# Holding the convolution for one period at the end of the last batch's mixing, and shifting it by one period from there on

## The chip, the cores and the metric

The kernel runs on one core of a Trainium2 chip. The metric is the device time of one execution in microseconds (us): the median of several runs. A profiled execution beside them gives the trace from which all durations below are read. Engines: PE is TensorE, DVE VectorE, ACT ScalarE, POOL GpSimd, SP the engine that issues nearly all DMAs here.

## The reference

The input `x` has 4 images of 256 x 256 positions and 64 channels, in float32. Layer 0 is a residual block, layer 1 a linear map along the image height:

```
h  = layernorm(x) @ w_te                          64 -> 128 channels
F  = fft2(h);  fc = gelu([Re F, Im F] @ w_fc)      the mixing, 256 -> 256
x1 = x + real(ifft2(fc)) @ w_tp                    128 -> 64
d  = gelu(depthwise_conv3x3(layernorm(x1) @ w_fe)) the convolution
x2 = x1 + d @ w_fp
out = moving average of x2 over the height + filtered rest   (layer 1)
```

Layer 1 is linear in the height and has its own weights per channel, so the kernel builds one 256 x 256 matrix for each channel and multiplies.

## The kernel before

**Stages.** The forward part turns columns of `x` into partial transforms and spills them to DRAM. The spectral part ("mixing") reads these, 65 pairs of frequencies per batch, transforms along the width, applies the weights and the gelu, projects, turns the result, and transforms back along the width (`u`, `us`, `uc`, `uf`: lines 849 to 924), which spills tensors `u_d` to DRAM. The convolution takes a batch in 32 chunks of 8 columns: it loads `uc` from `u_d` (`ul` or, for a batch's first chunk, `UL`, line 968) and a chunk of `x` (`xl`, line 1025), transforms back along the height (`s`, line 1034), adds to `x` (`r0`, `r1`), normalises (`c*`), turns to channels (`t`, `tt`), forms row sums on POOL (`T0`, `T1`), multiplies by the convolution weights (`gm`, `gh`, `em`, `eh`: lines 1166 and 1180), combines on DVE (`gc_`, `cf`, `ce`), applies the gelu (`a`), projects (`o`), turns back (`ft`) and stores (`st`, line 1314). Layer 1 follows when the last chunk is stored.

**Order.** The order of the instructions on PE, DVE, ACT and POOL is written out by hand; each engine runs its list in order. Time is cut into periods, numbered `n`. In each period the function `period` (line 1679) goes through a written list of pairs `operation:offset` and calls `do(operation, n + offset)`; `do` (line 1636) first calls what the operation depends on (`FOLLOWS`), so an operation that is asked for early pulls its predecessors forward, and one that was done already does nothing. There are four lists: `SPECTRUM`, `FULL` (forward, mixing and convolution), `MIXED` (mixing and convolution) and `CONV` (convolution alone, from period `CONV_FROM` = 171). SP's queue is not in these lists: its order is put together when the program is built.

**Chunks and periods.** `chunk_at` (line 1540) gives each chunk an index; in period `n` an operation with offset -k works on the chunk with index `n - k`. A convolution chunk is in flight for about 7 periods. A batch's first chunk needs the whole batch mixed, so it is set at `S0 + opened(b) + 2 + LATE` at the earliest. In numbers: batch 2 has the indices 137 to 168, batch 3 (the last) 170 to 201, and index 169 belongs to no chunk. Below, chunks 26 to 31 are those of batch 2, and 0', 1', 2' and so on those of batch 3. In period 169 the operations with offset 0 find no chunk, in period 170 those with offset -1, and so on to offset -6 in period 175: each stage skips once, one after the other.

**Late chunks.** From index `LATE_CHUNKS` = 167 (chunk 30) on, the products for the outer rows stay in PSUM and DVE adds them (`ce0`, `ce1`, line 1250). Earlier chunks have ACT copy them out (`ec`, line 1195) and POOL add (`sp`, line 1214).

**The end of the mixing.** The last two back transforms along the width, `u` with the numbers 131 and 132, stand in the periods 168 and 169. Their results are finished by `uf` 132 and `uf` 133 (one DVE instruction each, lines 920 and 907, and two DMAs each), which `UL` of chunk 0' calls in period 170. `UL` then loads the first columns, `first_column` (line 990) adds to them on DVE, and `s` of 0' (line 1041) reads them.

Of the kernel before, what the change touches and what calls it, by code (L numbers as in the profile page):

```python
# [136 lines left out]
def conv_seq_kernel(ctx: ExitStack, tc: tile.TileContext, a: dict, tables: bass.AP, out: bass.AP):  # L137
    nc = tc.nc
    x = a["x"]
    B = x.shape[0]  # L140
# [11 lines left out]
        em="ec1", o0="fs0", o1="fs1", ft0="st0", ft1="st1", y0="yt0", y1="yt1",  # L152
# [15 lines left out]
    def make_room(op):  # L168

        for other in list(taken):  # L170
            if len(free_banks) >= NEEDS.get(op, 1):
                break
            if other in taken:
                holder, k = taken[other][1]
                late = holder == "em" and k >= LATE_CHUNKS
                releaser = "ce1" if late else RELEASES[holder]
                if (releaser, k) not in pulling:
                    pulling.append((releaser, k))
                    do(releaser, k)
                    pulling.pop()  # L180
# [1299 lines left out]
    def x2_load(pool, c, b0, bufs):  # L1480
        xc = pool.tile([P, 2, BH, N // SW, CG, SW], F32, tag="xc", name=f"xc_{c}_{b0}", bufs=bufs)
        for b in range(BH):
            for t in range(2):
                nc.sync.dma_start(
                    xc[:, t, b], x2_d[b0 + b, t * P : (t + 1) * P, c // CG]
                )
        return xc
# [45 lines left out]
    S0 = FWD + 3  # L1533
    LATE = 1

    def opened(b):

        return (KH * (b + 1) + 2) // 2 + 1

    chunk_at, at = {}, 0  # L1540
    for b in range(B):
        at = max(at, S0 + opened(b) + 2 + LATE)
        for q in range(COLS):
            chunk_at[at] = (b, q)
            at += 1
    END = at + 6
    place = {chunk: at for at, chunk in chunk_at.items()}
    CONV_FROM = S0 + LATE + opened(B - 1) + 3

    def is_late(j):  # L1550
        return place[j] >= LATE_CHUNKS

# [21 lines left out]
    def numbered(text):  # L1574

        return [(w.split(":")[0], int(w.split(":")[1]) if ":" in w else 0) for w in text.split()]

    follows = {}
    for line in FOLLOWS.replace("\n", "|").split("|"):
# [15 lines left out]
    MIXED = numbered("""  # L1595
        xl:-1 XL:-1 ft0:-6 zs:-5 st0:-6 ft1:-6 st1:-6 em:-4 g0:-3 T1:-3 Ta:-3 eh:-4 zt:-6 ec0:-4
        ec1:-4 m1:-3 sp0:-5 sp1:-5 cx:-2 w:-5 cf1:-5 gc1:-3 g1:-4 b1:-3 cm:-1 cc:-2 UL t0:-2 a0:-5
        xs:-1 zt:-5 gm:-4 t1:-2 tt0:-2 a1:-5 p0:-4 p1:-4 z:-4 zs:-4 gh:-4 uf:-3 cM:-1 p0:-3 gc_0:-4
        cf0:-4 g1:-3 cp:-1 m1:-2 gc1:-2 b1:-2 s cl tt1:-2 r0 gc_1:-4 m0:-2 gc0:-2 m0:-1 p1:-3 z:-3
        gc0:-1 r1 x b0:-2 xs o1:-5 fs1:-5 u:-2 o0:-5 T0:-2 x:1 cq b0:-1 us:-2 fs0:-5 g0:-2 cr cR  # L1600
        uc:-2 w:-4 ul:1
    """)
# [4 lines left out]
        cm:-1 cc:-2 cM:-1 cp:-1 cf0:-4 tt1:-2 cf1:-4 tt0:-2 em:-4 eh:-4 T0:-2 T1:-2 cx:-1 fs1:-5 UL  # L1607
    """)

    LATE_CHUNKS = CONV_FROM + max(at for op, at in MIXED if op in ("em", "gm"))  # L1610

    FIRST = numbered("""
        v:1 mm:-2 fl:1 fM fr fm y0:-2 y1:-2 v:2 mm fq:1 fx:-1 fp fh1:-1 fh0:-1 fm:1 vc:1 yt0:-2 fq:1
# [22 lines left out]
    def do(op, index):  # L1636

        if op not in ops:
            return
        for k in range(done.get(op, -1) + 1, index + 1):  # L1640
            for other, at in EARLY.get(op, ()) if k < LATE_CHUNKS else ():
                do(other, k + at)
            for other, at in follows.get(op, ()):
                do(other, k + at)
            if op in ("u", "zt") and ring[0](op, k):
                do(*ring[0](op, k))
            if op in ("fq", "cq", "cc") and sq_user:
                user = sq_user[-1][0]
                do(user, done[user[0] + "q"])
            if op in RELEASES:  # L1650
                make_room(op)
            if done.get(op, -1) >= k:
                continue
            done[op] = k
            busy.append((op, k))
            if op in PAIRS:
                if op == "x" and k < B * KH - 2:
                    do("yt0", (k + 3) // KH * FWD + FWD - 1)
                    do("yt1", (k + 3) // KH * FWD + FWD - 1)
                if k < B * KH:  # L1660
                    ops[op](k)
            elif op in BACK:
                ops[op](k)
            elif op in MATRICES:
                if k < C:
                    ops[op](k)
            elif op in HALF_MATRICES:
                if k < 2 * BESIDE:
                    ops[op](k)
            elif op in forward:  # L1670
                if k < B * FWD:
                    ops[op](k)
            elif k in chunk_at:
                if op == "UL" and chunk_at[k][1] == 0:
                    do("uf", opened(chunk_at[k][0]) + 1)
                ops[op](chunk_at[k])
            busy.pop()

    def period(n):
        if any(n - k in chunk_at for k in range(7)):  # L1680
            names = FULL if n < B * FWD + 4 else MIXED if n < CONV_FROM else CONV
        else:
            names = SPECTRUM
        joint["on"], joint["whole"] = names is FULL, names is SPECTRUM
        for op, at in names:
            base = n
            if op in PAIRS:
                base = 2 * (n - S0)
            elif op in BACK:
                base = n - S0  # L1690
            elif op in HALF_MATRICES:
                base = (n - S0 - HALF_MATRICES[op]) // 2
            do(op, base + at)

    def starting(n, prep):
# [6 lines left out]
    with in_order, ExitStack() as right:  # L1702
        with (
# [3 lines left out]
            forward = forward_h(fwd)  # L1707
# [3 lines left out]
            with ExitStack() as early:  # L1711
                pool = early.enter_context(tc.tile_pool(name="matrices", bufs=2, side="right"))
                prep = early.enter_context(tc.tile_pool(name="prep", bufs=1, side="right"))
                ops |= matrices(pool)
                do("fl", 1)
                nc.sync.dma_start(tab, tables[:, :_L0_END])
                pieces = prepare(prep)
                next(pieces)
                nc.sync.dma_start(b_fp, row(a["b_fp"]).to_broadcast([P, C]))
                for n in range(S0 // 2):  # L1720
                    starting(n, pieces)
                for _ in pieces:
                    pass
                do("yt0", FWD - 1)
                do("yt1", FWD - 1)
                load_group(0)
                for k, names in enumerate(BETWEEN, C - BESIDE - len(BETWEEN)):
                    do("v", k)
                    do("vc", k)
                    do("mt", k - 1)  # L1730
                    for op, at in names:
                        do(op, S0 - 1 + at)
                do("mt", C - BESIDE - 1)
                begin(0)
                ops |= spectrum
                early_end = S0 + 4 * BESIDE + 1
                for n in range(S0, early_end):
                    if n == early_end - 3:
                        give_back()
                    period(n)  # L1740
# [4 lines left out]
            for n in range(early_end, S0 + LATE + opened(B - 1) + 2):  # L1745
                period(n)
        with tc.tile_pool(name="seq", bufs=1, side="left", reuse_waits="tile") as seq:
            mts = [matrix_load(seq, c) for c in range(0, CG, CM)]
            xc = x2_load(seq, 0, 0, 1)
            for n in range(S0 + LATE + opened(B - 1) + 2, END):  # L1750
                period(n)
            right.close()
            with tc.tile_pool(name="seq2", bufs=1, side="right", reuse_waits="tile") as seq2:
                for c in range(0, C, CG):
                    if c:
                        mts = [matrix_load(seq, c + i) for i in range(0, CG, CM)]
                    for b0 in range(0, B, BH):
                        if c or b0:
                            xc = x2_load(seq2, c, b0, 3)
                        layer1(c, b0, mts, xc, seq)  # L1760
# [39 lines left out]
```

## Time and profile before

| what | value |
|---|---|
| runs | 4324.39, 4318.21, 4323.12 us; median 4323.12 |
| profiled execution | 4325.4 us, of which the span of the trace is 4323.6 |
| busy over the span | PE 96%, DVE 80%, POOL 73%, ACT 68% |
| granted TensorE clock | 0.984 of full speed over the span |

A view by stretches gives the busy time of each engine between two times of the span. A timeline lists instructions that stand together: start, duration, engine, line, operation, tiles, and in square brackets how long the engine stood idle before and what ended that. A line of the matmuls of `s`, line 1041, marks each period: chunk 30's starts at 3290.64 us, 31's at 3313.56, 0's of the last batch at 3360.50.

### The profile page before, as it was taken

The numbers are of one execution on the slowest core, as the hardware profiler recorded it, in microseconds if no ns is written. First come the engines' busy times: TensorE is split into PE (matmuls) and PEld (weight loads), VectorE is DVE, ScalarE is ACT, GpSimd is POOL, SyncE is SP. The second block draws the span as 40 slices with busy tenths as digits, with TensorE's granted clock in tenths as the row PEclk, the third lists the DMA queues.
The fourth block names the chain that finished last, engine by engine and source line by source line (L and its number), as shares of the span: only waits on it lengthen the run. The fifth ranks groups of instructions, "written<-read, shape, count | busy, mean of one in ns | idle before, by whom it ended". The sixth has DMA issues, their size and how long they took to land.

```text
span 4323.6 us, 67389 instructions
## 1 busy us (share of the span) xinstructions
PE 4158.0 (96%) x22443; PEld 2315.2 (54%) x22443; DVE 3453.4 (80%) x5234; ACT 2961.5 (68%) x5409; POOL 3163.4 (73%) x3156
## 2 busy tenths in 40 slices
PE   8999999899999999899999999999998899999999
PEld 4544444345555555455555566666665566654444
DVE  6968999779999998899999878888887799962222
ACT  3338998678888887788888777888885466641111
POOL 6869999688888887788888877888887588840000
PEclk9999999989999999999999999999999999999999
DMA  6664555535454544444444443344433544439995
GB/s 190 211 190 142 161 161 162 152 98 137 137 137 137 137 137 124 122 122 138 138 138 129 113 109 109 106 112 112 118 98 91 173 113 118 114 108 358 342 343 228
DMA packets 763906, 655.28 MB, mean 152 GB/s; under 512 B 46413, under 2 KB 657695, under 8 KB 755240
## 3 DMA queue, kind: packets, MB, share of 16 engines
q1 hardware_dynamic: 726696, 583.84, 46.5%
q10 hardware_dynamic: 36864, 67.13, 4.1%
q8 instruction: 180, 2.95, 0.3%
q14 instruction: 166, 1.36, 0.1%
HBM read 364.81 MB, written 286.00 MB: 151 GB/s over the span
## 4 chain that ended last, share of the span: by engine, by line
PE 42%; POOL 6%; DVE 4%; DMA 4%; ACT 3%; issue 1%; SPq 1%; ACTq 0%; POOLq 0%; DVEq 0%
PE ps_o L1504 9%; PE ps_h_c L1166 5%; PE ps_p L750 3%; PE ps_s_c L1041 3%; PE ps_h_c L1180 3%; PE ps_f_c L1283 3%; PE ps_hh_c L1166 2%; PE ps_z L805 2%; PE ps_t_c L1088 2%; PE ps_u L856 2%; PE ps_x L725 2%; PE ps_ft_c L1308 2%; DMA out_dram<-oc 1%; PE ps_zt L823 1%; POOL xb L609 1%
## 5 line engine op out<-in xcount | busy, mean ns | idle before, releaser
L770 DVE TENSOR_TENSOR g<-ps_p,g 128x512 f32<-128x512 f32 x1040 | 702.2, 683 | 127.9 <-ACT g L764 109.7
L781 POOL TENSOR_TENSOR g<-g 128x512 f32<-128x512 f32 (+1 forms) x520 | 677.9, 1315 | 98.5 <-ACT g L775 88.8
L775 ACT ACTIVATE g<-g,b_fc 128x1024 f32<-128x1024 f32 (+1 forms) x520 | 598.3, 1151 | 1.5 <-DVE g L770 1.4
L750 PE MATMUL ps_p<-xs,wp 64*128 64x512 f32 (+1 forms) x2080 | 561.1, 615 | 9.9 <-DVE g L770 2.7
L1166 PE MATMUL ps_h_c<-td,wc_main 128*128 128x256 f32 x2048 | 517.1, 391 | 7.3 <-DVE s_c L1234 0.8
L764 ACT COPY g<-ps_p 128x512 f32<-128x512 f32 (+1 forms) x520 | 298.0, 585 | 268.5 <-PE ps_p L750 101.1
L1504 PE MATMUL ps_o<-xc,mt 128*128 128x512 f32 x1024 | 443.3, 595 | 3.9 <-DVE oc L1518 3.8
L1166 PEld LDWEIGHTS ps_h_c<-td,wc_main 128*128 128x128 f32 x2048 | 370.1, 193 | 122.5 <-ACT zt L833 36.7
L1276 ACT ACTIVATE h_c<-h_c,b_conv 128x1024 f32<-128x1024 f32 x256 | 297.6, 1164 | 140.6 <-DVE h_c L1245 54.1
L1518 DVE TENSOR_SCALAR oc<-ps_o,b_fp 128x512 f32<-128x512 f32 x128 | 93.5, 749 | 351.4 <-DMA out_dram<-oc 196.7
L1516 ACT ACTIVATE oc<-ps_o,b_fp 128x512 f32<-128x512 f32 x128 | 86.2, 686 | 363.0 <-PE ps_o L1504 196.7
L1128 POOL TENSOR_TENSOR td<-tt 128x512 f32<-128x512 f32 x256 | 327.0, 1299 | 10.0
L1504 PEld LDWEIGHTS ps_o<-xc,mt 128*128 128x128 f32 x1024 | 195.3, 191 | 251.2 <-issue 236.0
L609 POOL TENSOR_TENSOR xb<-xt 128x512 f32<-128x512 f32 x224 | 285.4, 1282 | 54.5 <-DVE xt L602 41.1
L750 PEld LDWEIGHTS ps_p<-xs,wp 64*128 64x128 f32 x2080 | 189.3, 186 | 239.6 <-issue 84.7
L805 PE MATMUL ps_z<-g,w_tp 128*64 128x512 f32 x1024 | 288.7, 617 | 24.6 <-POOL g L781 19.9
L725 PEld LDWEIGHTS ps_x<-tab,yb 128*64 128x64 f32 x4064 | 235.0, 138 | 133.3 <-issue 69.2
L1322 DVE TENSOR_TENSOR st<-x_c,ps_ft_c 128x256 f32<-128x256 f32 x512 | 261.8, 602 | 44.4 <-PE ps_ft_c L1308 41.4
L615 PE MATMUL ps_y<-xb,tab 128*64 128x512 f32 x1024 | 273.4, 623 | 23.3 <-POOL xb L609 17.1
L1283 PE MATMUL ps_f_c<-h_c,w_fp 128*64 128x512 f32 x1024 | 266.3, 615 | 15.6 <-ACT h_c L1276 15.5
L1180 PE MATMUL ps_h_c<-td,wc_half 64*128 64x256 f32 (+1 forms) x2048 | 278.6, 396 | 2.4 <-POOL td L1132 1.1
L1041 PE MATMUL ps_s_c<-uc_c,tab 64*128 64x512 f32 x1024 | 259.6, 616 | 15.6 <-DVE uc_c L990 8.7
(201 smaller groups left out, 9559.4 us busy)
## 6 DMA issues: line engine op xcount, KB each, us to landing
y_d<-yt SPq DMA_DIRECT2D x256, 256.0 KB, 3.6
yb<-y_d SPq DMA_DIRECT2D x256, 256.0 KB, 4.0
u_d<-ut SPq DMA_DIRECT2D x256, 256.0 KB, 3.6
x_c<-in_x_dram SPq DMA_DIRECT2D x512, 128.0 KB, 3.6
x_d<-st SPq DMA_DIRECT2D x128, 512.0 KB, 5.1
xc<-x_d SPq DMA_DIRECT2D x64, 1024.0 KB, 8.5
out_dram<-oc ACTq DMA_DIRECT2D x256, 256.0 KB, 5.8
xt<-in_x_dram SPq DMA_DIRECT2D x504, 128.0 KB, 2.5
```

What stands on the lines that cost most here:

```text
L609: engine.tensor_tensor(sums[j][:, i], x0, x1, (ALU.add, ALU.subtract)[i])
L750: nc.tensor.matmul(ps[:, :nf], wp[rows, cols], rhs[rows], start=True, stop=r == 1 or not pr["special"],)
L770: nc.vector.tensor_tensor(gt[:, i], re, gt[:, 1], op)
L775: nc.scalar.activation(g, g, AF.Gelu, bias=b_fc[:, half : half + 1])
L781: nc.gpsimd.tensor_tensor(g[:, 0], g[:, 0], g[:, 1], op)
L805: nc.tensor.matmul(ps[r * C : (r + 1) * C, :nf], w_tp, d[:, :nf], start=True, stop=True)
L1041: nc.tensor.matmul(pss[i], tb[i * C : (i + 1) * C], uc[i * C : (i + 1) * C, ::-1, 1 - r, :] if down else uc[i * C : (i + 1) * C, :, r, :], ...
L1128: tt_(new[:, k : k + 3 : 2], a_c, nb_e, op)
L1166: nc.tensor.matmul(product(j, k, par), wc_main[:, par, k, :], td[:, k, slots(j)].rearrange("p j q -> p (j q)"), start=k in (0, 1, 3), stop ...
L1180: nc.tensor.matmul(product(j, k, par)[:, dst.start * Q : dst.stop * Q], wc_half[lo : lo + C, k, :], td[lo : lo + C, k, src].rearrange("p j ...
L1283: nc.tensor.matmul(ps[par * C : (par + 1) * C], w_fp, gs[j][:, :, par, i0 : i0 + 2, :].rearrange("p r j q -> p r (j q)"), start=True, stop ...
L1504: nc.tensor.matmul(ps[:, :nf], mts[i // CM][:, i % CM, t, to * P : (to + 1) * P], xc[:, t, :, :, i, :], start=t == 0, stop=t == 1,)
```

## The change

A list `HOLDS` is added with one period in it, 36 + 132 = 168. In that period and in all later ones the operations of the convolution are called with the index `n - 1 + offset` in place of `n + offset`; those of the forward part, the mixing and the matrices keep theirs. So in period 168 every operation of the convolution is asked for a chunk that it did in period 167, and nothing of the convolution is issued. The chunks of batch 3 get the indices 169 to 200, with no free index before them, so their operations stand in the same periods as before: `s` of 0' in period 170. The chunks of batch 2 that are in flight in period 168 do each of their remaining steps one period later. `LATE_CHUNKS` becomes 166: chunk 29 is now treated as a late one. `END` stays 208.

```diff
+    HOLDS = [S0 + LATE + opened(B - 1)]
     chunk_at, at = {}, 0
     for b in range(B):
-        at = max(at, S0 + opened(b) + 2 + LATE)
+        at = max(at, S0 + opened(b) + 2 + LATE - sum(n <= S0 + opened(b) + 2 + LATE for n in HOLDS))
         for q in range(COLS):
             chunk_at[at] = (b, q)
             at += 1
-    END = at + 6
+    END = at + 6 + len(HOLDS)
...
-    LATE_CHUNKS = CONV_FROM + max(at for op, at in MIXED if op in ("em", "gm"))
+    LATE_CHUNKS = (
+        CONV_FROM - len(HOLDS) + max(at for op, at in MIXED if op in ("em", "gm"))
+    )
...
     def period(n):
-        if any(n - k in chunk_at for k in range(7)):
+        if any(n - k in chunk_at for k in range(7 + len(HOLDS))):
             names = FULL if n < B * FWD + 4 else MIXED if n < CONV_FROM else CONV
...
                 base = (n - S0 - HALF_MATRICES[op]) // 2
+            elif op not in forward:
+                base = n - sum(held <= n for held in HOLDS)
             do(op, base + at)
```

What this makes of the engines' lists, read from the two built programs (up to chunk 30's `s`, and again from chunk 5' on, they are the same):

- PE: the eight matmuls of `u` 131 come right after those of `u` 130, and `u` 132 takes 131's old place, between the `o` matmuls of chunk 26. `s` of 0' follows the products of chunk 28; before it followed those of 29. From there to 5' each period has all stages, in the order `s, ft, gm, ft, o, gh, t, t, em, eh`; before, the stages of the missing index were absent one by one.
- DVE: the first `uf` instruction of `u` 130 (line 920) and the two of `uc` 131 come before the `st` of chunk 25; lines 920 and 907 of `uf` 132 and 133 come right after the variance of chunk 31. Chunk 29 gets four instructions of `ce`.
- ACT: `us` 131 comes before the boundary copy (`Ta`, line 1138); two copies (`ec`) of chunk 29 are gone. POOL: four additions (`sp`) of chunk 29 are gone.
- SP: the stores of `uf` 130, 131, 132 and 133 each move forward; the store of `st` 12 and the load of `x` for 31 stand around those of 130 and 131. In the refill, the load of chunk 1' now stands wholly after the store of `st` 13; four loads of layer 1's matrices (0.5 MB each) stand together ahead of the load of `x` for 2', and the small store `fix_d` stands between the two halves of that load.

## The prediction

> **What bounds the kernel now.** I read the page first. Its row of slices (each about 108 us) shows PE at 90% or more nearly everywhere, and low in two neighbours, slices 31 and 32, from 3243 to 3459 us.
>
> ```profile
> span 4323.6 us, 67389 instructions
> ...
> PE   8999999899999999899999999999998899999999
> ```
>
> That is where the mixing ends and the last batch's convolution starts. The view by stretches, cut at the starts of `s` (line 1041), comes next; its columns are stretch, length, then busy time and count of PE, PE's weight loads, DVE, ACT, POOL, then granted clock and DMA.
>
> ```profile
> 3223.74:3246.50 22.76, 22.76 (x150) 14.68 (x150) 19.10 (x29) 19.07 (x35) 19.00 (x23) 1.00 0.22 62
> 3290.64:3313.56 22.92, 18.42 (x91) 12.15 (x89) 14.69 (x24) 10.48 (x22) 14.43 (x21) 0.85 0.44 115
> 3313.56:3360.50 46.94, 34.75 (x171) 22.93 (x167) 28.11 (x46) 20.92 (x41) 27.91 (x34) 0.89 0.37 102
> 3360.50:3444.88 84.38, 68.27 (x336) 42.88 (x338) 63.42 (x113) 36.84 (x72) 50.24 (x82) 0.90 0.56 181
> 3444.88:3514.20 69.32, 68.59 (x396) 47.08 (x394) 66.07 (x119) 43.23 (x83) 57.34 (x84) 1.00 0.39 107
> ```
>
> With mixing a period takes 22.8 us and PE is full. After the mixing's pairs are done (3290 on) it still takes 22.9 with no engine full: the written order, not work, sets it. From chunk 0' to 5' (3360.50 to 3444.88) five periods take 84.4 us though their stages are thinned out; the next five, complete, take 69.3, PE full and DVE at 95%. The timeline of PE shows the waits inside.
>
> ```profile
> 3304.50 1.12 PE L1088 MATMUL ps_t_c<-ident,xn_c 128*128 128x128 f32 x4 [3.33 <-POOL xn_c L410]
> 3305.41 3.62 PE L1166 MATMUL ps_h_c<-td,wc_main 128*128 128x256 f32 x8
> ...
> 3349.11 1.11 PE L1088 MATMUL ps_t_c<-ident,xn_c 128*128 128x128 f32 x4 [3.75 <-POOL xn_c L410]
> ...
> 3360.50 3.01 PE L1041 MATMUL ps_s_c<-uc_c,tab 64*128 64x512 f32 x8 [2.28 <-DVE uc_c L990]
> ...
> 3404.43 3.68 PE L1283 MATMUL ps_f_c<-h_c,w_fp 128*64 128x512 f32 x8 [5.77 <-ACT h_c L1276]
> ```
>
> Each period waits some 3.3 us for POOL's `xn`, and the matmuls after it run at half speed (3.62 us; the same eight take 1.89 at 3298). The chain of waits (start, duration, what) tells what 0' waited for.
>
> ```profile
> 3347.92 0.60 DVE h_c L1245
> 3348.51 1.63 DVE ut L920
> 3350.16 0.61 SPq L896
> 3350.82 3.69 DMA u_d<-ut
> 3355.05 4.71 DMA first<-u_d
> 3359.86 0.55 DVE uc_c L990
> 3360.50 2.95 PE ps_s_c L1041 x7
> ```
>
> So the last mixing result goes DVE line 920, store, load, line 990, `s`: 12.0 us, and its start is set by DVE's list, behind the combine of chunk 28.
>
> [...]the shortest `x` load takes 2.7 us to land, and SP's loads of line 1030 did stand for the buffers of `st`.
>
> **The change, step by step.** All times are in the profiled execution's span.
>
> *The hold.* Before, period 168 cost a whole 22.92 us row of convolution. In the new list it holds `u` 131, `us`, `uc` and `uf` 130 only. PE: +1.72 us (eight matmuls of line 856) after 3296.0. There PE stood 1.17 us for `fs` anyway, so `ft` of 25 comes 0.6 late, and chunk 27's products end at 3301.7 in place of 3301.2; then PE waits for `xn` 29 until 3304.5, which POOL makes from inputs that are long ready. Net on PE: 0. DVE: line 920 (1.1) and `uc` (1.3) now stand ahead of `st` 25, which starts at 3300.4 in place of 3298.0; behind it stand the combine of 26 (ends 3306.2, was 3303.9), the variance, line 907 and the seed (3308.6, was 3306.3). What waits for these: ACT's gelu of 26 and the `tt` copies behind it (to 3309.8; ACT was next needed at 3312.95), and POOL's ten small operations, 3308.7 to 3311.7 (POOL was next needed at 3314.67). SP: the `x` load of 31 has its second half behind the store of 131, issued about 3310, landing about 3314, wanted at 3315.5. So `s` of 31 still starts at 3313.6: the hold costs nothing while these covers of 1.5 to 3 us stand, at most about 2.5 us if they don't.
>
> *The chain to 0'.* `u` 132 now stands where 131 stood (3316.28). DVE reaches the variance of 31 at 3326.76 as before and then line 920 of `uf` 132 at 3327.9, where line 907 stood; before it was 3348.4. The 12.1 us behind it are the same instructions and DMAs with the same neighbours: `s` of 0' at 3340.0 in place of 3360.5. Gain 20.5 us. One period of about 22 us is gone, and nothing that it did is left out: it goes into the refill.
>
> *The refill.* Before, 0' to 5' took 84.4 us: 68.3 of PE, part of that at half clock (granted 0.90). New matmuls in it: the stages of one chunk, `t` 1.1, products 7.6, `o` 1.9, `ft` 0.9, about 11.5 us; the idle is 16.1. Period by period: (1) 0' to 1' was 19.86; now the transposes of 31 stand in it, +1.1: 20.9. (2) 1' to 2' was 15.19, set by DVE, whose list there (13.4 us, plus nine instructions of the first chunk, about 1.9) is unchanged: 15.2. (3) 2' to 3' is a complete period: 13.9, from the rows after 3444 (69.3 / 5). (4) 3' to 4' has chunk 31, whose gelu waits for the edge addition (line 1269). Before, `o` came 8.9 us after `s` (3395.55 to 3404.43); a complete period has 6.3 us of matmuls between (3444.88 to 3451.18), so 2.6 us stay: 16.5. (5) 4' to 5' has the edge of 0': 3427.20 to 3435.72, 8.5, less 6.3: 16.1. Sum 82.6; gain 1.8. Chunk 29 as a late one puts 1.6 us on DVE in (1), behind 29's combine and ahead of `r0` of 1', which by this count is then 1 us late; POOL loses 2.9 us and ACT 1.1, which were not on the path. From 5' on the lists are the same, and layer 1 starts when the chunks end, so what is gained stays.
>
> *Sum.* 20.5 + 1.8 = 22.3 us. The profiled execution, 4325.4, becomes 4303.1; that one is 2.3 above the median of the runs, 4323.1, which becomes **4300.8 us**.
>
> Unknown: how PE's clock falls in the refill. At best all five periods take 13.9 and (1) 20.9: 76.5, gain 28; at worst the 11.5 us of added matmuls find no idle: 84.4 + 11.5, gain 9. I take the middle because the waits of (4) and (5) are in the trace.
>
> **Rivals.** *Loads come late (gain 10 to 15).* Layer 1's first 6 MB (four matrices, four 1 MB loads of `xc`) are issued at about 3335 to 3341. `x` of 1' is now issued wholly behind `st` 13's store, about 3356, wanted at 3362.5; two loads of 2' stand behind `fix_d`, about 3374, wanted at 3379. For it: `x` loads took up to 13.7 us to land between 3355 and 3400, with a median of 5.2. Against: by 3356 the 6 MB, at the 417 GB/s of the stretch 3360 to 3370, are 15 us gone. Price about 8 us, and a restart at half clock: 4310.
>
> *The refill is full (gain 28):* 4295. For it: PE has enough matmuls to keep its clock. Against: the edge chunks.
>
> *Nothing is gained.* The chain to 0' doesn't set the end; the thinned stages had slack that paid for the wait, so a full refill gives back what the hold saves: the added matmuls plus stalls of 10 us. 4321. Against: PE stands idle 16.1 us there, and DVE 21.
>
> *Slower: the clock stays down.* A PE that idles 4.6 us before `s` of 0' and 2.5 in (4) and (5) may run the refill at a low clock. At a granted 0.66, the worst 10 us stretch of before (3400 to 3410), instead of full speed, 62 us of matmuls after 1' cost 32 more: -22.3 + 32, 4333. It turns the sign below about 0.74 over the whole refill. Against: each fall in the trace is over in 3.6 us, and the thinner refill had 0.90.
>
> **How the numbers follow.** Likeliest (4295.5 to 4307) 0.60; late loads (4307 to 4314) 0.17; full refill (4290 to 4295.5) 0.09; nothing gained (4314.5 to 4331) 0.09; slower 0.05. A measurement here can tell about 0.2%, 8.6 us, from no change: faster, below 4314.5, is 0.86, same 0.09, slower 0.05. The range leaves out half of the full refill and the last two: 4292 to 4315.
>
> **What would show it.** `s` of 31 at the same time as before, 3313 to 3316: the hold is free. `s` of 0' near 3340, after a chain with line 920 at 3328. From 0' to 5' 80 to 86 us, PE's idle mostly ahead of line 1283 twice. `s` of 5' near 3422.6, and a period of 13.9 from there. Wrong if `s` of 31 slips by 3 us or more, if `r0` (line 1054) waits for DMAs, or if PE's clock in the refill is under 0.85.

## The result, and the profile after

| | before | after |
|---|---|---|
| median of 8 runs each | 4320.48 us (4318.21 to 4324.39) | 4304.24 us (4294.02 to 4307.89) |
| profiled execution | 4325.4, span 4323.6 | 4307.88, span 4306.1 |

The ratio of the times is 0.9959, with a 95% interval of 0.9948 to 0.9969: 16.2 us are gained, where 22.3 were forecast. The profiled executions differ by 17.5. The time lies in the forecast range, 3.4 us above the predicted 4300.8. The gain is short by more than that, by 6.1 us, because before's own median over eight runs is 2.6 us lower than that over the three from which the forecast started.

The page of the changed kernel, its span and PE's row of slices:

```profile
span 4306.1 us, 67386 instructions
...
PE   8999999989999999899999999999998899999999
```

The low pair is still in slices 31 and 32, so the page can't say what happened there. The view by stretches can. It is cut again at the starts of `s` (line 1041) of chunks 30, 31, 0' and 5', and then over the next five periods; the columns are stretch, length, busy time and count of PE, PE's weight loads, DVE, ACT and POOL, the granted clock, the DMA share and GB/s.

```profile
3290.59:3314.48 23.89, 20.12 (x99) 12.78 (x97) 17.02 (x27) 10.96 (x23) 15.33 (x21) 0.86 0.50 132
3314.48:3340.01 25.53, 17.50 (x91) 11.31 (x87) 17.81 (x29) 12.26 (x25) 16.93 (x24) 0.90 0.40 110
3340.01:3429.26 89.25, 78.91 (x408) 51.29 (x410) 73.18 (x131) 43.89 (x85) 58.22 (x88) 0.91 0.59 187
3429.26:3498.50 69.24, 68.72 (x398) 47.23 (x396) 66.32 (x119) 43.39 (x83) 57.28 (x84) 1.00 0.39 107
```

Chunk 30 to 31 took 22.92 us and takes 23.89: the period into which the hold falls is 0.97 longer. Chunk 31 to 0' took 46.94 and takes 25.53: 21.4 gained. The refill, 0' to 5', took 84.38 and takes 89.25: 4.9 lost, and 6.65 more than the forecast 82.6. The five complete periods after it are the same. At 5' the change is 15.6 us ahead. Small differences outside this region, which differ from execution to execution, make up the rest of the 17.5.

The timeline of PE in the changed kernel shows where the refill lost it (start, duration, line, what, count, and in brackets the idle time before and what ended it):

```profile
3305.36 1.11 PE L1088 MATMUL ps_t_c<-ident,xn_c 128*128 128x128 f32 x4 [3.77 <-POOL xn_c L410]
3306.27 3.62 PE L1166 MATMUL ps_h_c<-td,wc_main 128*128 128x256 f32 x8
...
3340.01 3.79 PE L1041 MATMUL ps_s_c<-uc_c,tab 64*128 64x512 f32 x8 [3.64 <-DVE uc_c L990]
...
3400.96 3.68 PE L1283 MATMUL ps_f_c<-h_c,w_fp 128*64 128x512 f32 x8 [3.79 <-ACT h_c L1276]
...
3420.10 3.50 PE L1283 MATMUL ps_f_c<-h_c,w_fp 128*64 128x512 f32 x8 [2.50 <-ACT h_c L1276]
...
3435.56 1.94 PE L1283 MATMUL ps_f_c<-h_c,w_fp 128*64 128x512 f32 x8
```

The two `o` groups of the edge chunks 31 and 0' (line 1283) wait for the gelu and then run 3.68 and 3.50 us. The same group takes 1.94 us in the next period, where nothing is waited for. The granted clock is 0.50 from 3399.85 to 3406.68 and from 3420.33 to 3423.75, and 1.00 over the five periods from 3429.26. (The counts are of records; a matmul of the kernel's text leaves two, so x8 stands for four.) The chain of waits of the changed kernel (start, duration, what) tells what the first of them waited for.

```profile
3334.87 4.43 DMA first<-u_d
3339.38 0.54 DVE uc_c L990
3340.01 3.80 PE ps_s_c L1041 x8
...
3389.59 4.64 DMA x_c<-in_x_dram
3394.36 1.22 DVE x_c L1054
...
3397.58 1.12 DVE h_c L1269
...
3399.77 1.14 ACT h_c L1276
3400.96 3.68 PE ps_f_c L1283 x8
```

The chunk of `x` for 3' lands late, at about 3394.2. `r0` (line 1054) waits 1.25 us for it, and in DVE's list the edge addition of chunk 31 (line 1269) stands behind `r0` and `r1`. The gelu and `o` follow.

### The profile page after: what moved, and what is told of

Same layout as the page of the kernel before. It is cut to its first block, busy times and chain, and to the rows that moved or that the text cites. A ratio compares the mean times of both kernels' runs of the same rounds, so it can differ in the third digit from the quotient of the medians.

```text
span 4306.1 us, 67386 instructions
## 1 busy us (share of the span) xinstructions
PE 4152.0 (96%) x22443; PEld 2317.2 (54%) x22443; DVE 3454.7 (80%) x5238; ACT 2961.2 (69%) x5407; POOL 3154.7 (73%) x3152
## 3 DMA queue, kind: packets, MB, share of 16 engines
q1 hardware_dynamic: 726696, 583.84, 46.7%
## 4 chain that ended last, share of the span: by engine, by line
PE 42%; POOL 6%; DVE 4%; DMA 3%; ACT 2%; issue 1%; SPq 1%; ACTq 0%; POOLq 0%; DVEq 0%
PE ps_o L1504 9%; PE ps_h_c L1166 5%; PE ps_p L750 4%; PE ps_s_c L1041 3%; PE ps_h_c L1180 3%; PE ps_f_c L1283 3%; PE ps_hh_c L1166 3%; PE ps_z L805 2%; PE ps_u L856 2%; PE ps_x L725 2%; PE ps_t_c L1088 2%; PE ps_ft_c L1308 2%; PE ps_zt L823 1%; DMA out_dram<-oc 1%; PE ps_hh_c L1180 1%
## 5 line engine op out<-in xcount | busy, mean ns | idle before, releaser
L615 PE MATMUL ps_y<-xb,tab 128*64 128x512 f32 x1024 | 273.6, 624 | 21.4 <-POOL xb L609 15.5
L1041 PE MATMUL ps_s_c<-uc_c,tab 64*128 64x512 f32 x1024 | 259.3, 614 | 18.1 <-DVE uc_c L990 11.2
```

The source lines that it names most:

```text
L1041: nc.tensor.matmul(pss[i], tb[i * C : (i + 1) * C], uc[i * C : (i + 1) * C, ::-1, 1 - r, :] if down else uc[i * C : (i + 1) * C, :, r, :], ...
```

## Experiments

The theory: the gain is the period removed by closing the free index; the hold is only what makes this possible without a cost; and the refill gives some back because the edge chunks' `o` is late and then runs at a lowered clock. All kernels below compute the whole output. In those with added matmuls, the products are overwritten. Line numbers are shifted by some lines in those kernels (`o` is line 1292 in those with a fill ahead of it). Times of `s` come from the timeline of PE of each kernel's profiled execution, each with a start of its own, so only intervals are compared.

### The hold alone

The free index 169 is kept, so that a period is held but none is removed; the chunks' treatment is that of before.

```diff
-        at = max(at, S0 + opened(b) + 2 + LATE - sum(n <= S0 + opened(b) + 2 + LATE for n in HOLDS))
+        at = max(at, S0 + opened(b) + 2 + LATE)
...
-    CONV_FROM = S0 + LATE + opened(B - 1) + 3
+    CONV_FROM = S0 + LATE + opened(B - 1) + 4
```

(The two loops over periods are split one period later.)

> The hold alone: period 168 issues nothing of the convolution, but the free index stays, so batch 3 keeps the indices 170 to 201, chunk 0' starts in period 171 and the list MIXED lasts one period longer; 0' still has the thinned stages behind it. Theory (the hold is free because PE waits for xn there anyway, and the gain comes from closing the free index): s of 31 at most 1 us later than before, s of 0' 46 to 49 us after it as before, the time within 4 us of the kernel before (4318 to 4324). Rival (the gain comes from the hold, which brings u 131 and 132 and the finished transform forward): s of 0' earlier by 10 to 20 us, about 4305. Rival (an emptied period costs its time): 10 to 22 us slower, 4330 to 4342.

Measured: 4321.10 us (13 runs) against 4321.33, ratio 0.9999 (0.9991 to 1.0007). The starts of `s` for 31 and 0':

```profile
3311.03 1.88 PE L1041 MATMUL ps_s_c<-uc_c,tab 64*128 64x512 f32 x8
...
3357.73 3.07 PE L1041 MATMUL ps_s_c<-uc_c,tab 64*128 64x512 f32 x8 [2.29 <-ACT h_c L1212]
```

31 comes 23.5 us after 30 (before: 22.9), 0' 46.7 after 31 (before: 46.9), and 5' 84.35 after 0' (before: 84.4). The hold by itself neither costs nor gives anything that can be measured.

### The closed index alone

No hold; only batch 3 moves to index 169.

```diff
-        at = max(at, S0 + opened(b) + 2 + LATE - sum(n <= S0 + opened(b) + 2 + LATE for n in HOLDS))
+        at = max(at, S0 + opened(b) + 2 + LATE - (b == B - 1))
...
-    CONV_FROM = S0 + LATE + opened(B - 1) + 3
+    CONV_FROM = S0 + LATE + opened(B - 1) + 2
...
-            elif op not in forward:
-                base = n - sum(held <= n for held in HOLDS)
```

(The loops are split one period earlier, and `uc` 131 is called at the end of period 168.)

> The free index closed without a hold: batch 3 has the indices 169 to 200, every operation of batch 3 stands one period earlier, the list CONV begins one period earlier, and u 132 is pulled to the end of period 168. Theory: as with the change, s of 0' 24 to 28 us after s of 31, and the same time as the changed kernel within 4 us (4300 to 4308). Rival (the hold is what brings the gain): no gain, or under 5 us, 4316 to 4321, because the chain to 0' then waits for u 132.

Measured: 4305.45 us (5 runs) against 4321.33, ratio 0.9968 (0.9956 to 0.9981), which overlaps the change's own. The starts of `s` for 31 and 0':

```profile
3312.35 1.88 PE L1041 MATMUL ps_s_c<-uc_c,tab 64*128 64x512 f32 x8
...
3340.23 3.79 PE L1041 MATMUL ps_s_c<-uc_c,tab 64*128 64x512 f32 x8 [4.98 <-DVE uc_c L990]
```

Here 31 comes 21.74 us after 30 (which starts at 3290.61), and 0' 27.88 after 31, where the change has 23.89 and 25.53. The sums are 49.62 and 49.42: which of the two periods takes the tail of the mixing makes no difference. The refill is 89.2, as in the change. So the gain is the closed index. The hold is one way to write it, and moves some 2 us from one side of 31 to the other.

### Chunk 29 in the early form

The change also makes chunk 29 a late one. This run puts it back.

```diff
     LATE_CHUNKS = (
-        CONV_FROM - len(HOLDS) + max(at for op, at in MIXED if op in ("em", "gm"))
+        CONV_FROM + max(at for op, at in MIXED if op in ("em", "gm"))
     )
```

> The change with chunk 29 treated as an early chunk, as before: ACT copies its outer rows out and POOL adds, four DVE instructions of ce (1.6 us) are gone from 0' to 1'. Theory (DVE is not what ends the period from 0' to 1', PE is): s of 1' within 1 us, the time of the changed kernel within 3 us. Rival (the late form of 29 is part of the 6.6 us by which the refill was longer than forecast): 2 to 4 us faster than the changed kernel, 4300 to 4302.

Measured: 4308.26 us (9 runs) against 4321.33, ratio 0.9969 (0.9959 to 0.9978). The refill is 92.75 us, 3.5 longer than in the change; 1' to 2' alone takes 20.4 in place of 15.1, of which 3' to 4' gives 2.3 back. The reason is in the timeline of DVE of this kernel:

```profile
3363.20 0.69 DVE L1239 TENSOR_TENSOR ps_hh_c<-h_c,ps_hh_c 128x512 f32<-128x512 f32 x1 [3.72 <-ACT h_c L1212]
```

PE in turn waits for `xn`, which DVE's lateness delays, and then runs slowly:

```profile
3375.51 1.26 PE L1088 MATMUL ps_t_c<-ident,xn_c 128*128 128x128 f32 x8 [2.01 <-POOL xn_c L410]
...
3378.52 2.93 PE L1166 MATMUL ps_h_c<-td,wc_main 128*128 128x256 f32 x6 [0.90 <-DVE s_c L1234]
```

In the early form, DVE's combine of 29 stands 3.72 us for a copy by ACT (line 1212) that comes behind ACT's copies of the outer rows, and everything behind the combine in DVE's list is late. Neither the theory nor the rival of this run had this: the late form is worth some 3.5 us in the trace, though the medians, 4308.3 against 4304.2 and 4306.7 of the change, don't tell the two apart clearly (the intervals of the ratios overlap).

### Keeping PE busy ahead of the edge chunks' `o`

If the lost time is the clock, matmuls without a use that fill the wait must shorten it.

```diff
+        FILL = {(B - 2, NCH - 1): 14, (B - 1, 0): 10}
...
+            for _ in range(FILL.get(j, 0) if half else 0):
+                nc.tensor.matmul(
+                    ps[0:C],
+                    w_fp,
+                    wc_main[:, 0, 0:4, :].rearrange("p k o -> p (k o)"),
+                    start=True,
+                    stop=True,
+                )
```

> The change with matmuls that do nothing useful ahead of the first o of chunk 31 (14 of 512 columns, 3.0 us at full clock) and of 0' (10, 2.2 us), which are overwritten by the right ones. They fill part of the idle time in which PE waits for the gelu of an edge chunk (3.79 and 2.50 us). Theory (the waits cost a fall of PE's clock besides their own length: o of 31 took 3.68 us and o of 0' 3.50 in place of 1.94): the two o groups take 1.9 to 2.2 us, s of 5' comes 3 to 5 us earlier after s of 3', and the time is 3 to 5 us less than the changed kernel's, with runs closer together. Rival (only the length of the wait costs): the same time as the changed kernel within 1 us, or slower by what the added matmuls exceed the wait.

Measured: 4311.85 us (7 runs), ratio 0.9977 (0.9966 to 0.9987): slower than the change. The fill was sized wrongly, as the timeline of PE shows:

```profile
3394.67 11.80 PE L1284 MATMUL ps_f_c<-wc_main,w_fp 128*64 128x512 f32 x27
```

A matmul leaves two records, and the fourteen took 11.80 us (27 of their 28 records stand in this line), 0.84 each, where I had reckoned 0.216, about what one record takes in the traces (eight of line 856 in 1.72 us). The run says nothing on the clock. It was repeated with 4 and 2 matmuls in place of 14 and 10.

> The same fill, sized by what the first one measured (0.84 us for each matmul that writes one half of the bank, not 0.216): 4 matmuls, 3.4 us, ahead of the first o of chunk 31 and 2, 1.7 us, ahead of that of 0', against waits of 3.79 and 2.50 us. Theory (besides their length, the waits cost a fall of PE's clock): both o groups take about 2 us in place of 3.68 and 3.50, and s of 5' comes 34 to 36 us after s of 3' in place of 38.7: 3 to 5 us less than the changed kernel's time. Rival (only the length counts): 38 to 39 us there, the time within 1 us of the changed kernel.

Measured: 4299.36 us (5 runs) against 4320.92, ratio 0.9952 (0.9940 to 0.9965). PE's timeline:

```profile
3337.26 1.99 PE L1041 MATMUL ps_s_c<-uc_c,tab 64*128 64x512 f32 x8 [3.65 <-DVE uc_c L990]
...
3397.34 1.94 PE L1292 MATMUL ps_f_c<-h_c,w_fp 128*64 128x512 f32 x8 [0.22 <-ACT h_c L1277]
...
3413.72 1.94 PE L1292 MATMUL ps_f_c<-h_c,w_fp 128*64 128x512 f32 x8 [0.64 <-ACT h_c L1277]
```

Both `o` groups take 1.94 us, and 3' to 5' takes 34.25 us in place of 38.7. They start as late after the `s` of their period as in the change, 10.36 and 8.86 us in both kernels, so the waits' ends have not moved, and the 4.4 us are PE's speed behind them: this much of the refill's loss is the clock, which is granted at 1.00 over the refill here (3337.26 to 3421.23) and at 0.91 in the change. The first line shows something that was not edited: `s` of 0' waits as long as in the change (3.65 and 3.64 us) and yet takes 1.99 in place of 3.79. That brings 0' to 1' from 21.5 to 19.7.

### The edge addition ahead of `r1`

The other part of the delay is DVE's order: `a0` is called ahead of `r1`, so that line 1269 no longer stands behind line 1062.

```diff
-        ce0:-5 ul:-1 s:-1 cl:-1 xl:-1 XL:-1 r0:-1 ce1:-5 r1:-1 a0:-5 ft0:-6 st0:-6 cr:-1 gm:-4
+        ce0:-5 ul:-1 s:-1 cl:-1 xl:-1 XL:-1 r0:-1 ce1:-5 a0:-5 r1:-1 ft0:-6 st0:-6 cr:-1 gm:-4
```

> The change with the gelu ahead of r1 in the list CONV: of the four engines' lists only DVE's changes, in two places, where the edge addition (line 1269) of chunks 31 and 0' comes before the two instructions of r1 (1.2 us). Theory (PE's wait in 3' to 4' and 4' to 5' is ended by the edge addition, by way of ACT's gelu): both waits 1.2 us shorter, and each o group less slow; s of 5' 34 to 37 us after s of 3' in place of 38.7, the time 2 to 5 us under the changed kernel's. Rival (the wait is ended by the load of x for 3', which r0 waits for): the wait in 3' to 4' stays at 3.8 us, since r0 stands ahead of the edge addition all the same, and at most 1.2 us is gained in all.

Measured: 4299.78 us (5 runs) against 4320.92, ratio 0.9949 (0.9935 to 0.9962). PE's timeline at the two `o` groups:

```profile
3399.91 2.40 PE L1283 MATMUL ps_f_c<-h_c,w_fp 128*64 128x512 f32 x8 [2.44 <-ACT h_c L1276]
...
3416.56 1.94 PE L1283 MATMUL ps_f_c<-h_c,w_fp 128*64 128x512 f32 x8 [1.13 <-ACT h_c L1276]
```

The waits shrink from 3.79 and 2.50 us to 2.44 and 1.13, and the slow matmuls go with them; 3' to 5' takes 33.2 us. The cut in the waits, 1.35 and 1.37, brings 2.7 us of the 5.5; the other 2.8 are the two groups themselves, 1.28 and 1.56 shorter behind the shorter waits.

### The half products ahead of `o`

Work that is ready can fill the wait too: `gh` (line 1180) is put ahead of `o` in the whole list `CONV`.

```diff
-        ft1:-6 a1:-5 cq:-1 Ta:-3 cR:-1 o1:-5 o0:-5 gh:-4 st1:-6 t0:-2 gc_0:-4 fs0:-5 gc_1:-4 t1:-2
+        ft1:-6 a1:-5 cq:-1 Ta:-3 cR:-1 gh:-4 o1:-5 o0:-5 st1:-6 t0:-2 gc_0:-4 fs0:-5 gc_1:-4 t1:-2
```

> The change with gh ahead of o in the list CONV: PE does the 16 half products of the next chunk (1.9 us) before the o matmuls in every period from 171 on, in place of behind them; ACT's copies move with it. Theory (real work in the wait has the effect of the fill): the waits ahead of o fall to 1.9 and 0.6 us, the o groups run at full clock or nearly, s of 5' 34 to 36 us after s of 3'; periods without an edge chunk stay at 13.8 to 13.9. The time 3 to 5 us under the changed kernel's. Rival (o standing later delays fs, ft and st, so the buffers of x come free later, and each period waits for its load): periods of 14 to 15 us from 5' on, and a slower kernel by up to 30 us.

Measured: 4318.46 us (13 runs) against 4320.92, ratio 0.9994 (0.9986 to 1.0002): nearly the whole gain is lost. 3' to 5' takes 31.7 us, better still; but then every third period takes 15.7 us in place of 13.9. In PE's timeline of such a period:

```profile
3466.71 0.91 PE L1180 MATMUL ps_h_c<-td,wc_half 64*128 64x256 f32 x5 [1.15 <-ACT td L1138]
```

The half products now come before ACT has copied the boundary (line 1138). In its effect the rival came true, longer periods from 5' on, but through a copy on ACT and not through the loads that it had named. Why only every third period is hit is not known. The same with the edge addition ahead of `r1` as well:

> Both list edits together: gh ahead of o, and the edge addition ahead of r1. Theory: the waits of the two edge chunks are covered nearly whole (2.6 and 1.3 us, less 1.9): s of 5' 29 to 33 us after s of 3' in place of 38.7, the time 5 to 9 us under the changed kernel's, 4295 to 4299. Rival (the waits have another end, the load of x): no better than the better of the two alone.

Measured: 4314.41 us (21 runs), ratio 0.9986 (0.9980 to 0.9993). 3' to 5' takes 29.65 us, and every third period 15.7 as before.

### Both orders in two periods only

The two edits are kept, but only in periods 174 and 175, the two with the edge chunks.

```diff
+    moved = ("r1", -1), ("o1", -5), ("o0", -5), ("gh", -4)
+    EDGE = [w for w in CONV if w not in moved]
+    EDGE[EDGE.index(("a0", -5)) + 1 : EDGE.index(("a0", -5)) + 1] = moved[:1]
+    EDGE[EDGE.index(("cR", -1)) + 1 : EDGE.index(("cR", -1)) + 1] = moved[3], *moved[1:3]
...
+            if n - CONV_FROM in (3, 4):
+                names = EDGE
```

> The changed kernel with the two list edits (gh ahead of o, the edge addition ahead of r1) in the two periods 174 and 175 alone, in which the edge chunks 31 and 0' stand; all other periods as in the changed kernel. Theory (the two edits cover the waits of the edge chunks; elsewhere gh ahead of o costs 1.9 us in every third period): 3' to 5' 29.5 to 30 us in place of 38.7, from 5' on 13.8 to 14.4 as in the changed kernel, and the time 7 to 10 us less, 4294 to 4297. Rival (what the edits save is given back at 5' to 8', because gh of 2' then waits): 4301 to 4305.

Measured: 4298.26 us (4296.05 to 4303.29, 5 runs) against 4322.69, ratio 0.9944 (0.9932 to 0.9957). The view by stretches, 0' to 5':

```profile
3341.05:3420.47 79.42, 72.47 (x408) 48.89 (x410) 71.03 (x130) 43.64 (x85) 58.27 (x88) 1.00 0.63 206
```

The refill takes 79.4 us in place of 89.3 and the clock stays at 1.00; 3' to 5' is 29.6, and the periods from 5' on are 13.8 to 14.0, so nothing is given back there. The median lies 1.3 us above the time expected. Of the 9.8 us, 9.0 come from those two periods and 1.8 from `s` of 0', which again took 1.99 us (after a wait of 3.63), less 1.0 that 1' to 2' is longer. Until period 174 this kernel's lists are those of the change, so the 1.8 is no merit of the edit.

The changed kernel itself ran beside it, on the same chip.

> The changed kernel once more, without an edit, beside the other two on one chip. Theory: 4302 to 4307; where its trace has s of 0' at full clock (1.99 us), 0' to 1' takes 19.7 us and not 21.5.

Measured: 4306.69 us (4295.01 to 4308.76, 5 runs), ratio 0.9954 (0.9941 to 0.9968). Its trace repeats the first: 0' to 5' 89.27 us, `s` of 0' 3.78, the two `o` groups 3.68 and 3.50. Against this run the edit in two periods is 8.4 us faster by the medians, 10.6 by the spans of the profiled executions; the intervals of the two ratios still overlap.

### The same, with matmuls ahead of `s` of 0'

Three matmuls without a use are put into the wait ahead of `s` of 0', in the same form as the fill above.

```diff
+            for _ in range(3 if j == (B - 1, 0) else 0):
+                nc.tensor.matmul(
+                    pss[0][0:C],
...
```

> The same, and three matmuls without use (2.5 us, overwritten by the right ones) ahead of s of 0', where PE waits 3.64 us for the last transform. Theory (whether PE's clock falls after a wait of 3.6 us differs from run to run: s of 0' and the o of chunk 27 behind it took 3.79 and 2.67 us in the changed kernel's trace, 1.99 and 1.94 in that of the fill): with the wait cut to 1.1 us the clock doesn't fall there; 0' to 1' 19.7 us, the time 0 to 3 us under the kernel without the fill. Rival: no difference, or up to 1 us slower.

Measured: 4300.56 us (4291.34 to 4304.28, 5 runs), ratio 0.9943 (0.9931 to 0.9955), the same as without them. PE's wait fell to 0.92 us and `s` took 1.99; but in the profiled execution without the fill it took 1.99 too, so the pair doesn't tell what the fill is worth. 0' to 1' is 19.7 in both.

## Why the prediction was right or wrong

**The hold costs nothing: right.** The hold alone gave a ratio of 0.9999. In the change's own trace chunk 31 is 0.9 us late, inside the 2.5 allowed. The place was not among those named: POOL's line 1132 took 2.19 us at 3298.22 in place of 1.29, so `xn` of 29 began at 3303.41 instead of 3302.54. I had called its inputs long ready and the wait for it unmoved. In the trace of the change DVE has begun line 920 0.17 us before it, at 3298.05, which the hold had moved there. In before DVE runs line 1322 beside this addition (3298.25), and it takes 1.29. DVE's list moved as forecast (combine of 26 done at 3306.2, seed at 3308.6).

**The chain to 0': right.** `s` of 0' starts at 3340.01; the forecast was 3340.0. Two small errors cancel in it: line 920 of `uf` 132 came at 3328.80, not 3327.9, because 31 was 0.9 late, and the chain behind it took 11.2 us, not 12.1 (line 920 itself 1.22 in place of 1.63, the load of `first` 4.43 in place of 4.71). Counted from the `s` of 30, the closed index alone comes to the same within 0.2 us.

**The refill: the mechanism right, its terms (1), (4) and (5) too small.** By period, forecast and measured: (1) 20.9, 21.5; (2) 15.2, 15.1; (3) 13.9, 14.0; (4) 16.5, 20.6; (5) 16.1, 18.0. Together 82.6 and 89.25.

Terms (4) and (5) were built as a complete period of 13.9 plus the lateness of `o`, 2.6 and 2.2. That leaves out what a wait does to the matmuls behind it. The line was in front of me: in the profile of before, `o` of 31 is shown with 3.68 us, and a complete period's with 1.94 could have been set beside it. I priced the wait and not the slow group after it, 1.7 in (4) and 1.6 in (5), nor the half products behind it, which in (4) took 1.65 and 1.25 us against 1.22 and 1.03 in (5). The fill of 4 and 2 matmuls took the slow groups away and brought 3' to 5' to 34.25, near the 32.6 forecast. The other part of (4) is 1.25 us of `r0` waiting for `x` of 3'. This is the late-loads rival at a small size, and at 3' rather than at 1' or 2', where it was expected; `r0` waiting for a DMA had been named as a sign of error.

Term (1) is 0.6 over because `s` of 0' ran 3.79 us; where it ran 1.99 in other kernels, the period took 19.7, which is 1.2 under. I took before's 19.86, with an `s` of 3.01, as it stood. The late form of 29 was counted in (1) as a cost on DVE, and ACT's copies as off the path; the run with the early form shows the reverse, since DVE there waits for ACT.

**The length of a wait doesn't tell what follows it.** 2.50 us of idle were followed by 3.50 in place of 1.94, while 3.63 to 3.65 us ahead of `s` of 0' were followed by 1.99 in six traced kernels (both fills, the edge addition first, half products first, both, both in two periods) and by 3.78 or 3.79 in the change (twice) and in the early chunk 29. (The longer wait of the closed index alone, 4.98 us, was followed by 3.79 too.) What differs in the traces is where the wait lies. In those of before and of the change, the granted clock is 1.00 or 0.50, and its changes, 47 and 49, all lie whole multiples of 3.41 us apart; counted from the start of the span, these marks come about 1 us later in the change (a fall at 3303.30 in before, at 3304.27 in the change). Here are stretches between marks, with busy time and count of PE, granted clock, DMA share and GB/s; the first three lines are the change, the last two the fill of 4 and 2 (whose marks are an estimate, 3.41 us apart, that fits its PE timeline: a record of line 1167 takes 0.43 us there from about 3304.9 to 3308.3, and 0.22 before and after).

```profile
3335.00:3338.41 3.41, 1.37 (x14) 1.00 0.93 263
3338.41:3341.82 3.41, 1.81 (x4) 0.50 0.98 330
3416.92:3420.33 3.41, 0.91 (x8) 1.00 0.00 0
...
3332.18:3335.59 3.41, 1.43 (x14) 1.00 0.93 251
3335.59:3339.00 3.41, 1.74 (x8) 1.00 0.99 321
```

A mark cuts the wait ahead of `s` of 0' in two. In the change 2.04 us of it lie before the mark, PE is busy for 40% of that stretch, and 0.50 follows; with the fill 1.98 us do, PE is busy for 42%, and 1.00 goes on. The 2.50 us ahead of the second `o` lie whole in one stretch, busy for 27%, and 0.50 follows. In the traces of before and of the change there are 94 such stretches between about 3280 and 3440 us, 75 of them at 1.00. Behind 13 of these, all busy for 40% or less, comes 0.50; behind the other 62, all busy for 50% or more, 1.00 goes on. Elsewhere in the kernel the clock also fell behind busier stretches (77% from 222.04 to 225.45 us in the change), so the figures are of this region. It is a reading of the traces; no run moved the marks.

**What stays open.** The changed kernel's thirteen runs lie at 4294.0 to 4295.8 (three) and at 4303.4 to 4308.8 (ten). The step goes with the clock: the mean granted clock of the three is 0.988 to 0.990, that of the ten 0.985 to 0.987, and a difference of 0.002 over 4300 us is 8.6 us. Where in the kernel these runs differ is not known: none of the three was profiled, and the `s` that starts some 300 us before this region, in lists that are alike in all kernels, already starts between 3006.6 and 3019.7 us in eight profiled executions. What decides where the marks fall in an execution was not found either. The same step is in the medians of five runs by which the kernels above are compared, so the intervals in the traces are the firmer evidence.

**The rivals.** "Nothing is gained" and "slower" fell with the result: the granted clock over the refill was 0.91, above the 0.85 named as a sign of error. A full refill (76.5 us) did not come about, but with the order of two periods changed the refill reached 79.4, at a granted clock of 1.00, so the matmuls are there to keep the clock once the edge chunks don't wait. That each fall is over in 3.6 us, which was held against "slower", is not what the trace of before shows: in this region the clock stays at 0.50 for 3.41 or for 6.83 us at a time.

## What to carry to other kernels

Where the written order and not work sets a period, an empty slot in it can be taken out whole: the work that it had held goes into the waits of its neighbours, and what comes back is found at the chunks with an extra step. Price a wait of PE as the wait plus the slow matmuls behind it: here waits of 2.5 to 3.8 us cost 1.6 to 1.8 us more in the next group, or nothing; by the reading above it depends on how they lie to the marks at which the granted clock changed. An order that helps two odd periods can hurt all regular ones, so change the list for those periods alone.

## What the runs showed of the hardware that was not expected

- The 128x512 matmul into one half of the 64-column outputs takes 0.84 us when only that half is written (14 in 11.80 us, two records each; in the fill of 4 and 2, at a granted clock of 1.00, four take 3.65). In `o`, whose matmuls alternate between the two halves, four take 1.94 us, 0.49 each: 1.7 times as fast in alternation. That the added matmuls also write the same place again and again was not tested apart.
- After about the same 3.64 us of idle, the same group of `s` took 1.99 us in some profiled executions and 3.79 in others, with no step between. In the traces of before and of the change the granted clock changes only at marks 3.41 us or a multiple of it apart. 2.04 us of idle ahead of such a mark went with the slow case (the change), 1.98 us with the fast one (the fill of 4 and 2).
- POOL's addition at line 1132 takes 1.29 us in the median of 128 in the change's trace, and 2.19 in the one at 3298.22, beside which DVE runs line 920. That line reads two `ut` tiles and no PSUM. That it is the cause was not tested by a run that moves it alone.
